# Four graph layers on one core: zero products ahead of layer 0, the branch moved behind the last store, layer 0's first loads into idle places

## The chip, the cores and the metric

The kernel runs on one core of a Trainium2 chip. The metric is device microseconds of one execution, from start to end of the program. Three runs of the kernel before took 511.5, 512.31 and 513.35 us; the median is 512.31 us.

## The reference

Four layers run one after the other over one dense matrix `adj` of 3327 x 3327 (float32, most of it zero) and node features `x` of 3327 x 64. Each layer computes new features, adds them to the old ones, and normalises each row.

```python
def _layernorm(x, axis=-1, eps=1e-5):
    m = jnp.mean(x, axis=axis, keepdims=True)
    v = jnp.var(x, axis=axis, keepdims=True)
    return (x - m) / jnp.sqrt(v + eps)
...
# layer 0
neigh = jnp.matmul(adj, features)
deg = jnp.sum(adj, axis=1, keepdims=True) + 1.0
neigh = neigh / deg
data = jnp.concatenate([features, neigh], axis=-1)
return jnp.matmul(data, W.T)
...
# layer 1: each pair (i, j) of nodes has a factor of its own
log_ij = _logmap(x[:, None, :], x[None, :, :], c)
agg = jnp.einsum('ij,ijc->ic', w, log_ij)
transformed = agg @ weight + bias
...
# layer 2
h_neigh = (adj @ X + X) / deg
...
# layer 3: only the last 100 neighbours of a row count, each half as much as the next
mask = (adj != 0).astype(support.dtype)
rank = jnp.cumsum(mask, axis=1)
w = mask * jnp.where(pos > 0, DECAY ** (k - pos), 0.0)
out = w @ support + bias
```

## The kernel before

The nodes are padded to 3328 = 26 blocks of 128. The transposed matrix is stored in four column chunks of 832 targets, and each chunk in 13 pairs of source blocks; one load brings one pair (128 partitions x 2 x 832 float32, 832 KB) into one of four buffers named `adj`. A layer thus reads 52 pairs. Loads are issued by SyncE (SP) in program order, each as soon as its buffer is free.

Layer 0 goes through the chunks in the order 0, 3, 1, 2, and through the pairs of a chunk from 12 down to 0. For each pair TensorE does four aggregating products (`aggregate_pair`, L488; the profile counts two matmuls for each) of the features `x0w` with the pair, into one PSUM bank. VectorE turns the pair into a 0/1 mask (L514). For the chunks 0, 1 and 2 TensorE then counts the nonzeros along the sources (`count`, L560, twelve bfloat16 products into two PSUM tiles), ScalarE writes the counts as bytes into `rank` (L570), and VectorE carries the last count into the next mask (L546); layer 3 needs these ranks. Six masks of chunk 0 are left over (`L0_SPILL`) and counted while chunk 3, which has no count in layer 0, is aggregated. `heads` says ahead of which pairs the own features of the blocks are made: `own_features` (L692) multiplies up to seven blocks of `xt` by the weights and ScalarE copies the result to `x0w` and `xr` (L698, L699). The seven small weight loads (`load_weights`, L205 to L211) are issued by SP when chunk 0 has reached pair 7.

When a chunk is aggregated, its sums are copied (`keep_sums`, L471), transposed back by TensorE (L603) and worked into new features by `sums0` and `features0`, a step at a time beside the pairs of the next chunk; `transposes0` (L671, L677, L678) then brings them into `ut` and `wt`, the two operands of layer 1. For the last chunk `sums0` runs at once behind the pairs, on VectorE alone (L606 to L623), `features0` inside layer 1.

Behind layer 0 VectorE sums up how many nodes are too near to the origin for a short formula (L796), TensorE adds over the partitions (L798), VectorE writes the integer `n_near` (L799), and all engines load it and branch (L1657, L1659): at zero to `layer1_far` and layers 2 and 3, otherwise to `layer1_near` and a second copy of layers 2 and 3. The first two pairs of layer 1 are loaded ahead, into `sums`.

In `layer1_far` two blocks at a time are worked on: TensorE makes the inner products (L858), VectorE multiplies with the matrix (L869), ScalarE squares and adds a constant (L882, L883), GpSimd (POOL) multiplies (L884) or, for fewer of the blocks, VectorE does the last two steps in one (L877), and TensorE aggregates (L889), six blocks behind. The steps of the late `features0` of the last chunk are put between these. Layers 2 and 3 follow; `epilogue3` makes the last rows and SP stores them (L1543, L1548). A scheduler of the framework orders the instructions of each engine by the order of the program and its own estimate; `issue_after` pins one behind another.

## Time and profile before

| | |
|---|---|
| the profiled execution, its own time | 514.65 us |
| its span | 512.9 us |
| TensorE busy | 471.0 us (92%) |
| VectorE busy | 382.7 us (75%) |
| ScalarE busy | 345.3 us (67%) |
| POOL busy | 214.8 us (42%) |
| granted TensorE clock, mean | 0.989 |
| read from memory | 130.88 MB, 257 GB/s over the span |

The profiled execution is 2.3 us longer than the median of the timed runs. Times below are microseconds from the start of its span. PE is TensorE, DVE VectorE, ACT ScalarE, POOL GpSimd, SP SyncE; SPq and POOLq are the instructions that issue loads and stores. Layer 0's chunks end at about 44, 73, 107 and 149 us, layer 1 at about 343, layer 2 at about 465; the rest is layer 3, whose early part lies among layer 2. The engines' busy shares are means over these stages; what a change is worth is read in its own stage.

### The profile page before, as it was taken

What the parts mean: (1) busy time and instruction counts of PE and PEld (TensorE: products, weight loads), DVE (VectorE), ACT (ScalarE), POOL (GpSimd) and SP (SyncE); (2) the same over time, 40 slices, a digit from 0 to 9 for tenths busy, and PEclk for the clock granted to TensorE, in tenths of its full rate; (3) what the DMA queues carried; (4) which work ended last, traced back from release to release, by engine and by line L of the source; (5) the groups of instructions that cost most, each with busy time, mean ns of one, the idle gap of its engine ahead of it and who ended that gap; (6) DMA issues with size and microseconds to landing.
All of it is one profiled execution on the core that took longest, in us unless ns stands there. A gap on an engine that the chain in (4) does not pass through costs nothing.

```text
span 512.9 us, 7870 instructions
## 1 busy us (share of the span) xinstructions
PE 471.0 (92%) x2888; PEld 240.0 (47%) x2888; DVE 382.7 (75%) x690; ACT 345.3 (67%) x432; POOL 214.8 (42%) x191
## 2 busy tenths in 40 slices
PE   5999899998967999999999999999999998999892
PEld 3454344453432333443353344354465545466782
DVE  3475429969867989889979987988789487836773
ACT  1455546776777998879977986921278846569882
POOL 2000201102108996769866995900412043420563
PEclk9999999999998999999999999999999999999997
DMA  8899999988829778867876878579969888970003
GB/s 274 289 386 335 389 385 354 339 293 265 305 67 306 252 260 265 266 209 226 266 245 216 253 267 267 195 272 404 327 202 356 305 293 331 315 277 2 0 0 75
DMA packets 46289, 132.49 MB, mean 258 GB/s; under 512 B 7046, under 2 KB 7150, under 8 KB 46178
## 3 DMA queue, kind: packets, MB, share of 16 engines
q1 hardware_dynamic: 45714, 131.36, 74.7%
q0 software_dynamic: 384, 0.52, 0.4%
q8 instruction: 24, 0.39, 0.3%
q14 instruction: 23, 0.19, 0.1%
q10 hardware_dynamic: 144, 0.03, 0.0%
HBM read 130.88 MB, written 0.85 MB: 257 GB/s over the span
## 4 chain that ended last, share of the span: by engine, by line
PE 55%; DVE 20%; ACT 11%; DMA 7%; issue 3%; POOL 2%; POOLq 0%; DVEq 0%; ACTq 0%
PE one L488 13%; PE two L858 11%; PE one L889 10%; DMA adj<-in_adjt_dram 6%; PE two L560 5%; DVE mask L546 4%; PE two L488 4%; ACT s L882 3%; ACT s L883 3%; DVE mask L514 3%; PE two L1463 3%; DVE p L869 2%; DVE exponents L1362 2%; DVE s L877 2%; PE two L926 1%
## 5 line engine op out<-in xcount | busy, mean ns | idle before, releaser
L884 POOL TENSOR_TENSOR s<-s,p 128x832 f32<-128x832 f32 x70 | 135.5, 1956 | 34.7 <-DVE p L869 21.1
L869 DVE SCALAR_TENSOR_TENSOR p<-two,adj 128x832 f32<-128x832 f32 x100 | 101.7, 1020 | 15.0 <-issue 11.1
L570 ACT ACTIVATE rank<-two,last_bias 128x832 uint8<-128x832 f32 x78 | 71.9, 952 | 45.5 <-PE two L560 23.8
L858 PE MATMUL two<-uw 64*128 64x416 f32 x416 | 89.8, 546 | 8.7 <-DVE s L877 3.9
L889 PE MATMUL one<-s,xu 128*64 128x416 f32 x416 | 86.2, 525 | 0.0
L488 PE MATMUL one<-adj,x0w 128*64 128x416 f32 x416 | 82.6, 524 | 2.6 <-ACT x0w L698 1.4
L882 ACT ACTIVATE s<-two 128x832 f32<-128x832 f32 x70 | 60.1, 860 | 27.5 <-DVE p L869 27.0
L546 DVE SCALAR_TENSOR_TENSOR mask<-two,minus_last,mask 32x832 bf16<-32x832 f32 x48 | 52.5, 1093 | 32.9 <-PE two L560 28.9
L858 PEld LDWEIGHTS two<-uw 64*128 64x128 f32 x416 | 37.6, 188 | 60.5 <-PE one L889 16.9
L514 DVE TENSOR_SCALAR mask<-adj 128x1664 bf16<-128x1664 f32 x48 | 50.7, 1056 | 18.3 <-DMA adj<-in_adjt_dram 17.5
L883 ACT ACTIVATE s<-s 128x832 f32<-128x832 f32 x70 | 62.6, 897 | 1.8
L560 PE MATMUL two<-mask,tri 128*64 128x416 bf16 x416 | 53.1, 345 | 7.2 <-DVE mask L546 5.1
L488 PE MATMUL one<-adj,xr 128*64 128x416 f32 x264 | 54.5, 518 | 1.2 <-DMA adj<-in_adjt_dram 1.0
L889 PEld LDWEIGHTS one<-s,xu 128*64 128x64 f32 x416 | 26.0, 136 | 48.1 <-issue 41.7
L488 PEld LDWEIGHTS one<-adj,x0w 128*64 128x64 f32 x416 | 29.3, 139 | 34.5 <-issue 23.8
L560 PEld LDWEIGHTS <-tri 128*64 128x64 bf16 x416 | 25.8, 111 | 39.8 <-issue 24.4
L1384 ACT ACTIVATE bits<-rank 128x832 fp32r<-128x832 uint8 (+1 forms) x42 | 38.7, 986 | 6.2 <-PE one L488 3.6
L1380 POOL TENSOR_SCALAR bits<-exponents 128x832 fp32r<-128x832 bf16 (+1 forms) x20 | 24.4, 1237 | 37.1 <-PE one L1463 19.3
L877 DVE SCALAR_TENSOR_TENSOR s<-two,p 128x832 f32<-128x832 f32 x34 | 34.6, 1018 | 0.8 <-ACT two L874 0.5
L1463 PE MATMUL two<-bits,parts 128*128 128x416 f32 x144 | 30.7, 359 | 2.0 <-POOL bits L1380 2.0
L874 ACT ACTIVATE two<-two 128x832 f32<-128x832 f32 x34 | 28.8, 847 | 4.4 <-DVE p L869 3.6
L570 ACT ACTIVATE uw<-two,last_bias 128x832 uint8<-128x832 f32 x26 | 24.2, 950 | 11.1 <-PE two L560 5.9
(311 smaller groups left out, 538.0 us busy)
## 6 DMA issues: line engine op xcount, KB each, us to landing
adj<-in_adjt_dram SPq DMA_DIRECT2D x135, 832.0 KB, 6.0
uw<-in_adjt_dram SPq DMA_DIRECT2D x7, 832.0 KB, 6.1
a<-in_adjt_dram SPq DMA_DIRECT2D x8, 416.0 KB, 6.7
sums<-in_adjt_dram SPq DMA_DIRECT2D x2, 832.0 KB
p<-in_adjt_dram SPq DMA_DIRECT2D x4, 416.0 KB, 6.5
s<-in_adjt_dram SPq DMA_DIRECT2D x4, 416.0 KB, 7.5
uw<-in_xt_dram SPq DMA_DIRECT2D x1, 640.0 KB
out_dram<-o SPq DMA_DIRECT2D x2, 192.0 KB, 2.9
```

The source lines that it names most:

```text
L488: issued = nc.tensor.matmul(acc[h * D : (h + 1) * D, 0:HC], lhsT=x[:, 2 * jp + k, 0:D], rhs=a[:, bass.ts(h, HC)], start=(first and k == 1) ...
L514: issued = nc.vector.tensor_scalar(mask, a2, 0.0, None, op0=ALU.not_equal)
L546: ranks.carried = nc.vector.scalar_tensor_tensor(halves(last), ranks.after[P - 32 : P, :, 0:HC], minus_last[P - 32 : P, :], halves(last), ...
L560: issued = nc.tensor.matmul(counts[k][rows, h, 0:HC], lhsT=lhsT[:, rows], rhs=mask[:, of, bass.ts(h, HC)], start=lhsT is tri, stop=(k == 1 ...
L570: ranks.made = nc.scalar.activation(halves(ranks.rank[:, 2 * jp + k, :]), counts[k][:, :, 0:HC], AF.Relu, bias=last_bias,)
L858: issued = nc.tensor.matmul(v[:, h, 0:HC], lhsT=wt[rows, bass.ts(jb, P)], rhs=ut[rows, bass.ds(c * CH + h * HC, HC)], start=True, stop=True,)
L869: issued = nc.vector.scalar_tensor_tensor(halves(p), v, 0.25 - 0.5 * FD, halves(a), op0=ALU.add, op1=ALU.mult)
L882: nc.scalar.activation(halves(s), v, AF.Square, bias=FB - 0.5, scale=-2.0)
L883: nc.scalar.activation(s, s, AF.Copy, bias=FG)
L884: nc.gpsimd.tensor_mul(s, s, p)
L889: issued = nc.tensor.matmul(acc[h * D : (h + 1) * D, 0:HC], lhsT=xu[:, jb, 0:D], rhs=s[:, bass.ts(h, HC)], start=first, stop=last,)
L1463: issued = nc.tensor.matmul(acc3[c][h][:, 0:HC], lhsT=parts[:, 2 * jp + b, :], rhs=bits[b][:, bass.ts(h, HC)], start=(c not in begun and b ...
```

## The change

- Thirteen bfloat16 products of a zero tile, 128 x 416 each, are put on TensorE ahead of everything else; VectorE clears the tile first.
- Own features: two blocks and four blocks ahead of pairs 12 and 11 as before, then four blocks at a time, each behind the aggregation of a pair (10, 8, 6, 4, 2), into the PSUM bank `one1` in place of the tiles that the counts use.
- The pairs 8 to 0 of chunk 0 are loaded into places that are idle then (`sums`, the `wt` half of `uw`, and parts of `rank` of the chunks 1 and 2), so that these nine loads wait for no buffer. `load_weights` moves to POOL's queue.
- Spilled masks: the number left grows from 1 in place of 0, to 6 as before.
- `transposes0` of a chunk in layer 0 goes in two parts (four blocks, then the others) through the bank of the chunk's sums.
- For the last chunk, the addition of `xr` and the squares in `sums0` go to POOL; its small tiles lie in PSUM.
- `vote` (the former L796 to L799) comes at the end of `layer1_far`. The far way always runs; only behind the last store is `n_near` loaded and branched on, and at a nonzero count the near way computes all from layer 1 on again. For that `xr` is kept in memory by a store of 832 KB on POOL's queue in layer 1 (`kept_x1`), and the PSUM banks are opened once for all layers.
- In the last `epilogue3` the root lies in PSUM in place of SBUF.

```diff
+L0_IDLE = 13
...
     def load_weights():
-        nc.sync.dma_start(out=w1s, in_=w1)
-        nc.sync.dma_start(out=w2s, in_=w2.rearrange("(t k) f -> k t f", t=2))
+        nc.gpsimd.dma_start(out=w1s, in_=w1)
+        nc.gpsimd.dma_start(out=w2s, in_=w2.rearrange("(t k) f -> k t f", t=2))
...
+    kept = ctx.enter_context(tc.tile_pool(name="kept", bufs=1, space=bass.MemoryType.DRAM))
+    kept_x1 = kept.tile([P, NB, D], FP, name="kept_x1")
...
-        (nc.vector if last else nc.gpsimd).tensor_add(y, y, xr[:, b0:b1_, 1:D])
-        ss = ss_last[:, 0:nb] if last else Work(nb)("ss")
-        yield sum_of_squares(y, nb, ss, last)
+        nc.gpsimd.tensor_add(y, y, xr[:, b0:b1_, 1:D])
+        ss = work("ss")
+        yield sum_of_squares(y, nb, ss, nc.gpsimd if last else False)
...
+    far = ExitStack()
+    banks = Banks(far, "psum_far")
     with ExitStack() as l0s:
-        banks = Banks(l0s, "l0psum")
...
+        zeros = setup.tile([P, HC], BF, name="zeros")
+        nc.vector.memset(zeros, 0.0)
+        idle = banks.pair(1)
+        for _ in range(L0_IDLE):
+            nc.tensor.matmul(
+                idle[:, 0, 0:HC], lhsT=zeros[:, 0:P], rhs=zeros, start=True, stop=True
+            )
...
         def own_features(b0, b1_, behind):
             nb = b1_ - b0
-            ps = per_block(places.free(), nb, 2 * D)
+            ps = per_block(banks.one(1), nb, 2 * D)
...
-        heads = {12: (24, 26), 11: (20, 24), 9: (13, 20), 6: (6, 13), 2: (0, 6)}
+        heads = {12: (24, 26), 11: (20, 24)}
+        ahead_of_use = {10: (16, 20), 8: (12, 16), 6: (8, 12), 4: (4, 8), 2: (0, 4)}
...
+        rooms = [sums, wt] + [
+            rank[:, c, :, :].rearrange("p b i -> p (b i)").bitcast(FP) for c in ORDER[2:]
+        ]
+        rooms = [room[:, bass.ts(k, 2 * CH)] for room in rooms for k in range(room.shape[1] // (2 * CH))]
+        rooms = [room.rearrange("p (b i) -> p b i", b=2) for room in rooms]
+
+        def load_early(jps):
+            for jp in jps:
+                loaded[jp] = load_adj(ORDER[0], jp, rooms.pop(0) if jp < 9 else None)
+
+        load_early((9, 8))
...
+                if n == 0 and jp in ahead_of_use:
+                    issued = own_features(*ahead_of_use[jp], issued)
...
-                left = (L0_SPILL - jp // 2 if ranks else jp // 2) if n < 2 else L0_LAG
+                left = (min(L0_SPILL, L0_SPILL + 1 - jp // 2) if ranks else jp // 2) if n < 2 else L0_LAG
...
-                        transposes0(ORDER[n - 1], places.free(), counted or issued, True)
+                        for k0, k1 in ((0, 4), (4, GB)):
+                            bank = banks.one((n - 1) % 2)
+                            transposes0(ORDER[n - 1], bank, counted or issued, True, k0, k1)
...
+                if n == 0 and jp == 10:
+                    load_early((7, 6, 5, 4))
+                    load_weights()
                 if n == 0 and jp == 7:
-                    load_weights()
+                    load_early((3, 2, 1, 0))
...
-        vote = banks.one(NCH % 2)
-        nc.tensor.matmul(vote[0:1, 0:1], lhsT=nearest, rhs=ones, start=True, stop=True)
-        nc.vector.tensor_copy(n_near, vote[0:1, 0:1])
...
+    def vote(bank, behind):
         nearest = small.tile([P, 1], FP, name="nearest", tag="nearest")
         nc.vector.tensor_reduce(nearest, near, axis=AX.X, op=ALU.add)
+        issue_after(nc.tensor.matmul(bank, lhsT=nearest, rhs=ones, start=True, stop=True), behind)
+        nc.vector.tensor_copy(n_near, bank)
...
+                    if late is None and i == late_at:
+                        nc.gpsimd.dma_start(out=kept_x1, in_=xr)
...
-                own = {"ss": "s", "root": "a", "part": "var"} if ends_with else {}
-                def work(name, work=Work(nb)):
+                own = {"ss": "vn", "part": "var"} if ends_with else {}
+                def work(name, work=Work(nb, bank if ends_with else None)):
...
+    with far:
+        layers_2_and_3(banks, *layer1_far(banks))
     some_near = nc.values_load(n_near[0:1, 0:1], min_val=0, max_val=NP)
-    with tc.If(some_near == 0) as cmp:
-        with ExitStack() as arm:
-            banks = Banks(arm, "psum_far")
-            layers_2_and_3(banks, *layer1_far(banks))
-    with cmp.Else():
+    with tc.If(some_near > 0):
         done = layer1_near()
```

## The prediction

> **What bounds the kernel now.** I read the busy time by stage first, then the chain that ended last, then the order of time at four places. By stage (us, then busy us and count of PE, PEld, DVE, ACT, POOL, then granted clock, DMA share, GB/s):
>
> ```profile
> 0.00:16.00 16.00, 10.17 (x46) 5.82 (x48) 5.22 (x15) 4.15 (x7) 3.44 (x35) 1.00 0.88 291
> 16.00:44.00 28.00, 26.60 (x196) 14.33 (x194) 18.15 (x35) 12.96 (x19) 0.74 (x5) 1.00 0.94 328
> 44.00:73.00 29.00, 27.37 (x196) 12.64 (x194) 11.03 (x29) 16.85 (x21) 3.45 (x4) 1.00 1.01 381
> 73.00:107.00 34.00, 32.51 (x252) 15.56 (x250) 29.43 (x47) 22.67 (x28) 4.16 (x4) 1.00 0.97 342
> 149.50:168.00 18.50, 10.41 (x44) 4.31 (x46) 13.83 (x27) 12.07 (x15) 12.53 (x12) 0.91 0.86 286
> 168.00:344.00 176.00, 172.85 (x905) 73.20 (x905) 154.31 (x251) 143.65 (x181) 133.58 (x70) 1.00 0.75 244
> ```
>
> Chunk 3 (44 to 73) runs at the rate of the loads, 381 GB/s at a full share; chunk 0 moves only 291 and 328 GB/s. So a lead of the loads in chunk 0 is a lead through chunk 3. From 168 on TensorE is the bound. Between them, at 149.5, it stands. The chain of waits (start, us, what) says where:
>
> ```profile
> 11.73 2.08 PE two L560 x12
> 16.70 1.07 PE two L560 x12
> 17.80 1.10 DVE mask L546
> 18.92 0.95 ACT rank L570
> 19.88 0.43 ACT x0w L698
> 56.51 7.67 DMA adj<-in_adjt_dram
> ...
> 151.00 0.62 DVE ss_last L430
> 151.65 0.18 DVE near_nodes L615
> 151.84 0.19 DVE nearest L796
> 152.03 0.04 issue
> 152.08 0.20 PE one L798 x2
> 152.31 0.16 DVE n_near L799
> 152.46 1.14 issue
> 153.61 2.99 PE two L858 x8
> ```
>
> Twelve count products take 2.08 us at 11.73 and 1.07 later: the array is slow until about 13.6, and again at 153.61, where eight L858 take 2.99 against 1.6 elsewhere (granted clock 0.91 in that stage). At 17.8 own features wait behind a count for ScalarE. At 149.5 the last count product is done, and the first product of layer 1 begins at 153.61, behind the vote and the branch.
>
> **Part by part.** *Zero products.* One L560 pair takes 0.35 us slow, and I take a full-width product of 416 columns to be as long as such a pair (no row shows one): 13 x 0.35 = 4.5 us, from about 1.1 to 5.6, just ahead of the first own features at 5.83, which wait for VectorE's `w0r`, not for TensorE. Cost nothing, unless they run over. What they can save by 13.6: eight L488 at 2.97 against 1.40 and the 2.08 against 1.07, together 2.6 us. But the loads land at 6.3, 8.5, 10.9 and 16.0 there, and TensorE, once fast, waits for them. So I book no term of its own; it is inside the next one. [...]
>
> *Chunks 0 and 3.* In the trace pair 9 lands at 16.0, pair 0 of chunk 0 at 39.7, the last pair of chunk 3 at 70.6. Before, loads wait for one of four buffers, and SP spends 15.77 to 19.6 on weight loads:
>
> ```profile
> 11.77 3.95 SPq L311 DMA_DIRECT2D adj<-in_adjt_dram  x2
> 15.77 0.48 SPq L205 DMA_DIRECT2D w1s<-in_w_dram  x1
> ```
>
> With nine pairs free to go, loads follow at the rate of chunk 3 (45.7 to 70.6 for 11 pairs: 2.26 us a pair): pair 0 at 16.0 + 9 x 2.26 = 36.3, chunk 3's last at 65.7. TensorE from 16.0: ten pairs x 1.40 + six counts x 1.05 + 16 own blocks x 0.126 + 0.5 = 22.8, so 38.8; chunk 3 is 13 x 1.40 + 6 x 1.05 + 1.3 = 25.8, so 64.6 and with stalls about 66. Both meet near 66 to 67.1 (65.7 + 1.4) against about 72 (70.6 + 1.4). Own features in fours take away the waits on ScalarE at 17.8 to 20.3 and 37.0 to 37.5. Gain 5.5; bounds 3.5 (pair 0 no earlier than 36.3, none of it added in chunk 3) and 7. Chunks 1 and 2 have loads, masks and counts as before; a phase earlier, the same length.
>
> *Transposes in layer 0.* TensorE waits 0.64 and 0.85 us on ScalarE's copies at 104.6 and 143.0, and up to 1.7 at 69.1. Their own bank lets counts go on; ScalarE's second pair of copies adds some 0.3 a chunk. Gain 1.0; bounds 0 and 2.3.
>
> *POOL's queue in layer 0.* Seven weight loads and three last-row loads stand at its front, the reads of `rank` rows between its steps. A POOL issue took 0.5 to 0.7 us mostly, once 3.68, and a POOL addition twice its 0.93 beside L514:
>
> ```profile
> 117.61 1.98 POOL L612 TENSOR_TENSOR y<-y,xr 128x441 f32<-128x441 f32 x1 [21.23 <-DVE y L611]
> 130.37 0.93 POOL L647 TENSOR_TENSOR xu<-y,a 128x441 f32<-128x441 f32 x1 [4.45 <-DVE a L645]
> 360.53 3.68 POOL L591 DMA_DIRECT2D rank<-last_more  x1 [26.34 <-DVE last_more L589]
> ```
>
> Ten issues at the worst of these are 37 us, at 0.6 six; POOL's next work in before is at 41.6, and the weights are first read by VectorE at 36.2, behind pair 2's mask, which the lead brings to about 33. So the front costs nothing in the likely case (third rival). The read of chunk 1's rows waits for ScalarE's last count of chunk 1 (117.9) and is queued ahead of L612 at 117.61: VectorE's sum behind it already waits 0.49 there. Cost 0.4; bounds 0 and 0.9.
>
> [...]
>
> *Layer 1's start.* The vote and branch leave: 149.5 to 153.61 on TensorE is 4.1 us, and the slow restart 1.4. In their place stands a chain on POOL: ScalarE's last count (151.1), the read of the rows (0.51), the addition and the squares (0.93 each with VectorE idle; 1.98 beside L514, which is over by then), so 153.6. VectorE's sum of the squares (0.62) stands between the first and second L869, so every later L869 waits for it: second L869 done 155.3, near steps 0.35, third 156.7, fourth 157.7 against 159.66. ScalarE (1.75 a block) then ends block five's L874 at 163.15 against 165.2, VectorE's L877 follows at 164.2 against 167.63, and with it TensorE's unbroken run at 164.4 against 167.77. Gain 3.4. Bounds: 1.5 if both POOL steps take 1.98 (+2.1), 5.0 if TensorE keeps all of 4.1 and most of the restart. The second load into `sums`, issued 148.9 behind four others, lands near 153.5, ahead of the third L869.
>
> *The store of `xr`* is one POOL issue behind the ninth L884, ahead of the tenth. POOL is back to back there (eight L884 in 15.34 us), but by then blocks lie some 5 us ahead of TensorE. Cost 0.2; bounds 0 and 3.7. Its 832 KB are 2.3 us of a queue at 0.75 share. *The vote* at layer 1's end: 0.2 on TensorE ahead of L912 and 0.16 on VectorE ahead of L903: 0.15 (0 to 0.4). SP's load of `n_near` (0.5 to 0.75) stands where SP waits 11 us for buffers (363 to 374.6): nothing, 0.7 at worst.
>
> *The end.* Here L449 takes 0.89 in place of 0.16, beside POOL:
>
> ```profile
> 505.40 0.94 POOL L1536 TENSOR_TENSOR o<-twice,root 128x448 f32<-128x448 f32 x1
> 505.46 0.89 DVE L449 TENSOR_TENSOR var<-var,a 128x4 f32<-128x4 f32 x1
> ```
>
> With the root in PSUM it may not; but SP issues stores until 508.2 and the last store's landing (512.0) ends the program, so SP must follow. Gain 0.5; bounds 0 and 1.2. The new branch on the four engines and on SP lies beside that landing (3.2 us); 0, a microsecond at worst.
>
> Sum: -5.5 - 1.0 + 0.4 - 3.4 + 0.2 + 0.15 - 0.5 = -9.65. Against the profiled 514.65 that is 505.0; that execution is 2.34 above the median, so 512.31 - 9.65 = 502.7.
>
> **Rivals.** *First: the loads in chunk 0 can't go faster.* Their share is already 0.88 and 0.94 at 291 and 328 GB/s; if small or narrow transfers, not the buffers, hold them down, only about 1 of the 5.5 comes. Against it: the same chunk moves 363 GB/s from 28 on, and is slow where buffers and SP run dry. 512.31 - 9.65 + 4.5 = 507.2. *Second: POOL's chain takes the vote's place.* If its issue and two steps run into 156 or later, the 3.4 falls to 0: 502.66 + 3.4 = 506.1. For it: the 1.98 row. *Third, the slower one: weights come late.* VectorE's queue holds `turn` of w1 ahead of the masks near 33; if POOL's issues, starved by L514, bring w1 to b3 only at 33 + 9.65 = 42.7 or later, the change is slower, by as much as they are later; at ten issues of 3.68 from 4.3 plus 8 us of landing (the longest POOL row), 49: about 6 slower, 518.6. Against it: three last-row loads landed in 6 us each beside four running pairs, with issues of 0.5 to 0.7. *Fourth: the large terms do nothing* (first and second together, and chunk 3 keeps its pace): within 0.3% of 512.3.
>
> **How the numbers follow.** Forecast as summed, within 499 to 505: 0.54. First rival 0.16, second 0.16, third 0.06, fourth 0.03, slower by several bounds at once 0.02, faster than 499 (large bounds together: -7 - 2.3 - 5 - 1.2 = 496.8) 0.03. The range of 8 in 10 takes in the first two rivals and half of the rest: 498.5 to 509.5. About 0.3% (1.5 us) is what a measurement of this kernel can tell from no change. Faster by more than that: 0.54 + 0.16 + 0.16 + 0.03 = 0.89; same 0.03; slower 0.08.
>
> **What would show it.** Right: pair 0 of chunk 0 lands near 36 and chunk 3's last near 66; twelve L560 take 1.05 from the first; no gap over 1 us on TensorE at layer 0's end, clock 1.00 there; second L869 done near 149 (155.3 less the 6.1 of layer 0), layer 1 ending some 9 us earlier than 343; L449 at 0.16 in the last rows. Wrong: chunk 1 beginning no earlier than 70 (72 before), a long DVE wait on POOL or on a weight load near 33, or layers 2 and 3 longer than 169 us, where I book nothing and the scheduler has reordered some counts.

## The result: 1.4% slower

The changed kernel took 520.88 us (median of six runs), the kernel before 513.06 us beside it: a ratio of 1.0143, with a 95% interval of 1.0101 to 1.0185. I had forecast 502.7. The execution profiled was the longest of the six, 526.26 us with a span of 524.5; it is a slow run (mean granted clock 0.969, the five others 0.977 to 0.987), which the ratio leaves out. So the trace is read for where time went, and the ratio for how much.

The stages of the changed kernel, in the columns of the first view of before (us, then busy us and count of PE, PEld, DVE, ACT, POOL, then granted clock, DMA share, GB/s):

```profile
16.00:44.00 28.00, 24.29 (x172) 12.15 (x169) 17.98 (x34) 13.69 (x23) 0.61 (x4) 1.00 1.03 390
44.00:77.00 33.00, 30.85 (x206) 14.39 (x207) 11.82 (x29) 17.19 (x23) 3.60 (x5) 0.95 0.79 287
157.00:168.00 11.00, 8.34 (x28) 2.84 (x28) 8.07 (x19) 9.07 (x12) 9.27 (x6) 0.69 0.21 71
405.00:440.00 35.00, 31.17 (x188) 16.32 (x185) 23.89 (x45) 20.22 (x29) 10.61 (x12) 1.00 0.92 325
440.00:474.00 34.00, 33.62 (x181) 18.20 (x179) 17.52 (x39) 21.36 (x22) 9.31 (x10) 0.95 0.65 227
```

Chunk 0's loads do run faster, 390 GB/s in place of 328. The lead is then thrown away: chunk 3 moves 287 GB/s where it moved 381. And the granted clock, 1.00 from 13.9 us on in before except for one short stretch and the last rows, is under 1.00 in three of these five.

The clock itself shows where part of the time goes. In all traces here it changes only at multiples of 3.413 us after its first change (in before after 41, 1 and 102 of them, in the changed kernel after 12, 1, 33, 2, 52, 2, 26, 1, 15, 1 and 5). These are the stretches of the changed kernel just ahead of a slow stretch (one at half clock), and the slow stretches behind them (same columns):

```profile
41.49:44.90 3.41, 1.30 (x14) 0.89 (x16) 0.67 (x3) 2.32 (x4) 0.76 (x5) 1.00 1.01 382
44.90:48.31 3.41, 3.41 (x16) 1.50 (x14) 1.09 (x1) 1.42 (x2) 0.00 (x0) 0.50 0.10 37
157.54:160.96 3.42, 1.35 (x8) 0.30 (x4) 1.87 (x5) 1.97 (x3) 3.07 (x3) 1.00 0.35 141
160.96:167.78 6.82, 6.23 (x16) 2.20 (x16) 5.62 (x13) 6.76 (x9) 5.44 (x4) 0.50 0.08 11
437.43:440.84 3.41, 1.51 (x13) 1.31 (x12) 1.95 (x3) 1.44 (x4) 2.22 (x3) 1.00 0.54 209
440.84:444.26 3.42, 3.42 (x13) 1.36 (x14) 2.82 (x5) 2.89 (x5) 0.00 (x0) 0.50 0.02 5
492.05:495.46 3.41, 1.57 (x7) 1.05 (x6) 1.98 (x2) 2.60 (x2) 3.41 (x3) 1.00 0.00 0
495.46:498.88 3.42, 3.37 (x10) 3.22 (x11) 1.52 (x2) 0.95 (x2) 3.42 (x3) 0.50 0.00 0
```

TensorE was busy for 1.30, 1.35, 1.51 and 1.57 us of 3.41, under half, and the next stretch ran at half clock. Where TensorE is the bound, one such stretch costs about 1.7 us of products (an estimate: half of 3.41). I counted all full-clock stretches in the 20 traces of this study: of those with TensorE busy for less than half, 52 of 52 were followed by a slow one (7 of 7 in the profiles of before and of the change); between 0.50 and 0.55, 4 of 14; above 0.55, 8 of 2,794. One wait of 1.9 us (in the stretch from 437.43), or two of 0.97 and 0.86 us (in the one from 492.05), were enough. The changed kernel's profiled execution has seven slow stretches between its start and its last rows, the one of before has one.

The stages by marks that hardly depend on where a slow stretch falls, us each, for the profiled execution of each kernel (chunk ends at the first copy of the chunk's sums; layer 1's start up to its first aggregating product; "border" from its last one to layer 2's first; "rest" from the last L1267 to the end of the span):

| kernel | chunk 0 | chunk 3 | chunks 1, 2 | start of layer 1 | layer 1 | border | layer 2 | rest |
|---|---|---|---|---|---|---|---|---|
| before | 43.6 | 29.8 | 72.7 | 18.7 | 175.6 | 3.3 | 122.5 | 46.6 |
| the change | 47.8 | 31.4 | 72.2 | 16.5 | 174.8 | 5.8 | 127.4 | 48.6 |
| zeros alone | 45.9 | 30.1 | 72.4 | 18.7 | 175.6 | 3.3 | 121.8 | 47.3 |
| loads alone | 45.4 | 30.1 | 71.0 | 18.7 | 175.6 | 3.3 | 121.5 | 48.9 |
| branch alone | 48.0 | 30.9 | 71.5 | 15.5 | 176.1 | 5.4 | 125.5 | 47.3 |
| transposes and root alone | 43.5 | 29.9 | 72.6 | 19.9 | 175.6 | 3.5 | 122.6 | 47.6 |
| change, last rows' loads held | 46.5 | 30.2 | 72.2 | 14.4 | 180.2 | 5.8 | 125.2 | 48.6 |
| change, vote apart, weights later | 44.2 | 29.8 | 72.9 | 16.1 | 175.1 | 3.6 | 121.3 | 48.3 |
| change, all mends | 42.7 | 29.7 | 72.7 | 15.8 | 176.7 | 3.6 | 122.1 | 49.0 |

Three places lose: chunk 0 (+4.2) with chunk 3 (+1.5), the border with layer 2 (+7.4), and the rest (+1.9). One gains: the start of layer 1 (-2.2). The change with the last rows' loads held, an experiment below, is another profile of nearly the same kernel: it loses in the same places, and in layer 1 by its own edit.

In chunk 0 the order on TensorE (start, us, instruction, idle before it) shows the wait:

```profile
39.39 0.32 PE L728 MATMUL two<-w1h,basis 64*64 64x64 f32 x2
...
41.71 0.54 PE L566 MATMUL two<-mask,tri 128*64 128x416 bf16 x4 [0.23 <-DVE mask L552]
44.14 0.54 PE L566 MATMUL two<-mask,tri 128*64 128x416 bf16 x4 [1.88 <-ACT wl L743]
44.49 0.54 PE L566 MATMUL two<-mask,minus 128*64 128x416 bf16 x4
44.84 2.97 PE L494 MATMUL one<-rank,x0w 128*64 128x416 f32 x8
```

Pair 0 landed at 38.6, but its aggregation (L494) stands behind a count, and the count behind ScalarE's copies of the later weights (L728 wrote them into a pair of banks that the counts use). Then the clock was at half: 2.97 us for eight, where the eight at 39.87, at full clock, took 1.62.

### The profile page after: what moved, and what is told of

Read it like the earlier page. It is cut to its first block, busy times and chain, and to the rows that moved or that the text cites. A ratio compares the mean times of both kernels' runs of the same rounds, so it can differ in the third digit from the quotient of the medians.

```text
span 524.5 us, 7920 instructions
## 1 busy us (share of the span) xinstructions
PE 484.7 (92%) x2901; PEld 244.3 (47%) x2901; DVE 378.9 (72%) x690; ACT 346.9 (66%) x442; POOL 222.1 (42%) x201
## 4 chain that ended last, share of the span: by engine, by line
PE 54%; DVE 20%; DMA 8%; ACT 7%; issue 4%; SPq 2%; POOL 2%; POOLq 0%; DVEq 0%; ACTq 0%
PE one L494 13%; PE two L891 11%; PE one L922 9%; PE two L566 6%; DVE mask L552 4%; DMA adj<-in_adjt_dram 4%; PE two L494 4%; DMA rank<-in_adjt_dram 3%; DVE mask L520 3%; ACT s L915 3%; PE two L1499 3%; DVE p L902 2%; ACT s L916 2%; SPq L317 2%; DVE s L910 2%
## 5 line engine op out<-in xcount | busy, mean ns | idle before, releaser
L576 ACT ACTIVATE rank<-two,last_bias 128x832 uint8<-128x832 f32 x78 | 72.4, 952 | 47.4 <-DVE mask L552 33.6
L891 PE MATMUL two<-uw 64*128 64x416 f32 x416 | 91.8, 554 | 6.0 <-DVE s L910 2.9
L494 PE MATMUL one<-adj,x0w 128*64 128x416 f32 x344 | 72.3, 517 | 4.1 <-DMA adj<-in_adjt_dram 3.2
L891 PEld LDWEIGHTS two<-uw 64*128 64x128 f32 x416 | 37.1, 190 | 59.9 <-issue 28.4
L566 PE MATMUL two<-mask,tri 128*64 128x416 bf16 x416 | 57.3, 344 | 7.6 <-DVE mask L552 5.2
L494 PE MATMUL one<-adj,xr 128*64 128x416 f32 x264 | 56.5, 530 | 0.7 <-DMA adj<-in_adjt_dram 0.7
L520 DVE TENSOR_SCALAR mask<-adj 128x1664 bf16<-128x1664 f32 x39 | 41.7, 1072 | 18.9 <-DMA adj<-in_adjt_dram 18.4
L922 PEld LDWEIGHTS one<-s,xu 128*64 128x64 f32 x416 | 26.0, 136 | 48.6 <-issue 42.4
L494 PEld LDWEIGHTS one<-adj,x0w 128*64 128x64 f32 x344 | 26.0, 136 | 29.6 <-issue 19.4
L1499 PE MATMUL two<-bits,parts 128*128 128x416 f32 x144 | 32.4, 373 | 3.4 <-POOL bits L1416 2.0
L566 PE MATMUL two<-mask,minus 128*64 128x416 bf16 x208 | 31.8, 340 | 0.0
```

The source lines that it names most:

```text
L494: issued = nc.tensor.matmul(acc[h * D : (h + 1) * D, 0:HC], lhsT=x[:, 2 * jp + k, 0:D], rhs=a[:, bass.ts(h, HC)], start=(first and k == 1) ...
L520: issued = nc.vector.tensor_scalar(mask, a2, 0.0, None, op0=ALU.not_equal)
L566: issued = nc.tensor.matmul(counts[k][rows, h, 0:HC], lhsT=lhsT[:, rows], rhs=mask[:, of, bass.ts(h, HC)], start=lhsT is tri, stop=(k == 1 ...
L576: ranks.made = nc.scalar.activation(halves(ranks.rank[:, 2 * jp + k, :]), counts[k][:, :, 0:HC], AF.Relu, bias=last_bias,)
L891: issued = nc.tensor.matmul(v[:, h, 0:HC], lhsT=wt[rows, bass.ts(jb, P)], rhs=ut[rows, bass.ds(c * CH + h * HC, HC)], start=True, stop=True,)
L922: issued = nc.tensor.matmul(acc[h * D : (h + 1) * D, 0:HC], lhsT=xu[:, jb, 0:D], rhs=s[:, bass.ts(h, HC)], start=first, stop=last,)
```

## Experiments

**Each part alone, and the loads undone.** First, the zeros alone on the kernel before:

```diff
+        zeros = setup.tile([P, HC], BF, name="zeros")
+        nc.vector.memset(zeros, 0.0)
+        idle = banks.pair(1)
+        for _ in range(13):
+            nc.tensor.matmul(idle[:, 0, 0:HC], lhsT=zeros[:, 0:P], rhs=zeros, start=True, stop=True)
```

> The kernel before with the thirteen products of zeros and nothing else of the change. Theory L (the new order of layer 0's loads is what costs; the zeros only make the array fast early, at about 4 us instead of 13.9): the products of chunk 0 that took 2.97 us for eight take about 1.5 from 6 us on, but the loads set the pace, so the time is 510.5 to 513, chunk 1 begins at 70.5 to 72. Theory C (the loss of the change lies in slow-clock windows that follow short waits anywhere in the program, wherever the waits come from): the zeros change nothing behind 20 us, 511 to 514, with slow windows behind 20 us as before (one at layer 1's start and the end).

Measured: 515.69 us, ratio 1.0051 (1.0028 to 1.0074). The zeros cost. TensorE of this run, with what it waited for on VectorE and ScalarE:

```profile
14.29 1.80 PE L700 MATMUL two<-w0r,uw 64*128 64x128 f32 x14 [0.21 <-DMA uw<-in_xt_dram]
16.11 1.03 DVE L515 TENSOR_SCALAR mask<-adj 128x1664 bf16<-128x1664 f32 x1 [2.98 <-DMA adj<-in_adjt_dram]
17.17 1.09 DVE L547 SCALAR_TENSOR_TENSOR mask<-two,minus_last,mask 32x832 bf16<-32x832 f32 x1
18.30 0.95 ACT L571 ACTIVATE rank<-two,last_bias 128x832 uint8<-128x832 f32 x1 [3.58 <-DVE mask L547]
19.15 0.52 ACT L706 COPY x0w<-two 128x441 f32<-128x441 f32 x1
19.72 5.82 PE L489 MATMUL one<-adj,x0w 128*64 128x416 f32 x16 [3.64 <-ACT x0w L706]
```

The fast array had done all that it could by 16.1 us, waited 3.64 us, and its next sixteen products took 5.82 us at half clock; in before, slow until 13.9, the wait at that place was 0.84 and sixteen took 3.01. Pair 9 landed at 16.1, so TensorE itself did not wait for it, but for the own features: their copy stands on ScalarE behind that of a count, and this one behind VectorE's work, which did wait for pair 9. Chunk 0 ended 2.3 us later. Theory L was right that the loads set the pace, by this detour, and wrong that this makes early speed harmless.

Then the changed kernel with its loads undone:

```diff
-        heads = {12: (24, 26), 11: (20, 24)}
-        ahead_of_use = {10: (16, 20), 8: (12, 16), 6: (8, 12), 4: (4, 8), 2: (0, 4)}
+        heads = {12: (24, 26), 11: (20, 24), 9: (13, 20), 6: (6, 13), 2: (0, 6)}
...
-                loaded[jp] = load_adj(ORDER[0], jp, rooms.pop(0) if jp < 9 else None)
...
-        nc.gpsimd.dma_start(out=w1s, in_=w1)
+        nc.sync.dma_start(out=w1s, in_=w1)
```

> The changed kernel with layer 0's loading as before: four buffers and no early rooms, weights issued by SP, own features in groups of two to seven in a free pair of banks, the old allowance of waiting masks. Zeros, transposes by halves, the addition and squares on POOL, the vote and the branch at the end stay. Theory L: chunk 0 ends near 43.5 instead of 47.8 and chunk 1 begins near 72 instead of 77; about 5 us come back, 515 to 516.5. My prediction's reading (the loads are a gain of 5.5 and something else costs more): it becomes 5 us slower still, near 526. Theory B (the move of the vote and of the work at layer 0's end costs): 519 to 522, the start of layer 1 as late as in the changed kernel relative to chunk 1's begin.

Measured: 521.75 us, 1.0199 (1.0145 to 1.0253). Nothing came back: chunk 0 ended at 46.9, with a slow stretch behind a wait at 18 us. So undoing the loads alone gives nothing back, and theory B's range held; the zeros, and three loads that an experiment below turns up, were still there.

> The kernel before with only layer 0's loading of the change: loads into idle rooms, weights issued by POOL, own features in fours, one more waiting mask. No zeros, and vote, branch and layer boundaries as before. Theory L: chunk 0 ends 3 to 5 us later than in the kernel before, and with the array slow until 13.9 rather more; 516 to 519. My prediction's reading: chunk 1 begins at 66 to 68, 507 to 508.5. Theory B or C (this part is harmless by itself): 511.5 to 514.

The reverse edit on the kernel before measured 515.84 us, 1.0058 (1.0029 to 1.0086). The loads land earlier here, pair 0 at 37.1 against 39.7, and chunk 0 still ends at 45.4, behind a wait of 1.88 us for ScalarE's copy of the later weights.

The later weights moved out of chunk 0:

```diff
-                if n == 0 and jp == 2:
+                if n == 1 and jp == 10:
                     later_weights(mask)
```

> The changed kernel with one move: the work on the later weights (two products into a free pair of banks, its copies on VectorE and ScalarE) stands behind pair 10 of chunk 1 and not behind pair 2 of chunk 0. If the 1.88 us wait of a count on ScalarE's copy at 42.3 and the slow-clock window behind it (44.9 to 48.3) are what makes chunk 0 end late: chunk 0 ends at 43.5 to 45 instead of 47.8, chunk 1 begins at 73 to 74.5, and the time falls by 2.5 to 4 to 517 to 518.5. If TensorE's own work in chunk 0 and the later landing of its loads set it (products without a gap from 20.4 to 41.5 us): chunk 0 ends at 46.5 or later and the time is within 1 us of 520.9.

Measured: 517.47 us, 1.0111 (1.0069 to 1.0154). Chunk 0 ended at 43.9 in place of 47.8: the 1.88 us wait and the slow stretch behind it were what made it late. Yet 43.9 is no gain on 43.6, although all loads of chunk 0 had landed by 38.5. TensorE's own work fills chunk 0. The same kernel without the zeros:

> The run with the later weights moved, without the thirteen zeros. If the zeros pay once the loads run ahead: the array is slow until 11 to 14 us, chunk 0 ends 1 to 2.5 us later than 43.9, 518 to 520. If they cost here as they do alone (+0.5%, because the fast array runs out of loads and falls back for two windows): 515 to 516.5.

Measured: 518.14 us, 1.0128 (1.009 to 1.0167), chunk 0 at 44.2. Beside the early loads the zeros neither pay nor cost by what these runs can tell.

**The branch alone.** Vote, branch, POOL's addition and squares, store of `xr`, on the kernel before:

```diff
-        nc.tensor.matmul(vote[0:1, 0:1], lhsT=nearest, rhs=ones, start=True, stop=True)
...
+            own = banks.pair()
+            vote(own[0:1, 1, 0:1], summed)
...
-    some_near = nc.values_load(n_near[0:1, 0:1], min_val=0, max_val=NP)
-    with tc.If(some_near == 0) as cmp:
+    with far:
+        layers_2_and_3(banks, *layer1_far(banks))
+    some_near = nc.values_load(n_near[0:1, 0:1], min_val=0, max_val=NP)
+    with tc.If(some_near > 0):
```

> The kernel before with only the move of the vote, the branch and the work at layer 0's end (addition and squares of the last group on POOL, copy of its sums, store of xr, vote behind layer 1, branch behind the last store). No zeros, loads, transposes and last root as before. Theory M (several small prices, read off the first four runs): layer 1's start gains 2.4 to 3.4, the vote costs 1.0 at layer 1's end, layer 2 about 0.6 and often a slow-clock window of 1.7, the program's end 1.6; sum +0.5 to +2.5, so 512.5 to 515. The prediction's reading (-3.4 + 0.2 + 0.15, the branch beside the landing): 509.2. If the 6 us between the run with zeros alone and the run with loads undone are all of this part: 517 or more.

Measured: 518.65 us, 1.0124 (1.0094 to 1.0153), more than theory M allowed. It loses most in layer 0, whose code it shares with before until the last group. POOL's order of time, and TensorE's, in this run:

```profile
4.96 2.61 POOL L587 DMA_DIRECT2D last_a<-in_adjt_dram  x3
```

```profile
17.89 1.82 PE L698 MATMUL two<-w0r,uw 64*128 64x128 f32 x14
21.82 5.82 PE L491 MATMUL one<-adj,x0w 128*64 128x416 f32 x16 [2.11 <-ACT x0w L704]
```

In before these three loads of the last adjacency rows were issued from 153.9 on, right behind the branch. Without a branch ahead of them nothing held them, and they went to the front of POOL's queue, among layer 0's first pairs: pair 9 landed at 18.2 in place of 16.0, pair 7 at 22.7 in place of 20.3 (the expectation below calls it pair 8). TensorE waited 2.11 us and then ran 16 products in 5.82 us at half clock. The changed kernel has them at 10.50, behind its seven weight loads, and its pair 9 lands at 18.2 too.

So I held them back behind the store of `xr` in layer 1 (the fill of `last_more` likewise):

```diff
+            issued = nc.gpsimd.dma_start(out=a[k * NB : (k + 1) * NB, :], in_=adjt[c, :, P - 1, :])
+            issue_after(issued, held)
```

> The run with the move of the branch alone, and one thing more: POOL issues the three loads of the last adjacency rows (and the fill of the tile behind them) behind the store of xr, early in layer 1, in place of the first microseconds of the program, where they had slid once no branch stood ahead of them. Theory R (these loads lie among layer 0's first loads and delay them: pair 9 landed at 18.2 instead of 16.0, pair 8 at 22.7 instead of 20.3, TensorE waited 2.1 us and ran two slow windows): pair 9 lands near 16.0 again, chunk 0 ends at 43.5 to 45 instead of 48.0, chunk 2 at 146 to 147.5 instead of 150.4; 514 to 515.5 against 518.65. If the late chunk 0 of that run was chance: about 518 again. If POOL, back to back in layer 1, can't take six issues more: layer 1 lasts longer than 176.1 us.

Measured: 519.21 us, 1.0127 (1.0097 to 1.0157): the same time, by another way. Layer 0 is back, chunk 0 at 43.6 and chunk 2 at 144.3 in place of 150.4. But layer 1 lasts 179.3 in place of 176.1. POOL, and then TensorE:

```profile
176.24 1.97 POOL L889 TENSOR_TENSOR s<-s,p 128x832 f32<-128x832 f32 x1
178.13 0.53 POOL L589 DMA_DIRECT2D last_a<-in_adjt_dram  x1
178.66 0.51 POOL L592 DMA_DIRECT2D last_more<-rank  x1
179.18 1.96 POOL L889 TENSOR_TENSOR s<-s,p 128x832 f32<-128x832 f32 x1
```

```profile
185.71 1.67 PE L863 MATMUL two<-uw 64*128 64x416 f32 x8 [2.95 <-DVE s L882]
```

Six issues and a fill, some 4 us, now stand between POOL's back to back products, and TensorE waits 2.95 us where it had not waited. Of the 6.1 us won by the end of layer 0, 3.2 were lost again in layer 1. On the whole change the same hold:

> The changed kernel with the last rows' loads held back behind the store of xr and nothing else. Theory R: pair 9 lands near 16.8 instead of 18.2, pair 0 near 37.1 instead of 38.6; the count that waits for ScalarE's copy of the later weights at 42.3 still waits, so chunk 0 ends at 45 to 48; 518 to 520.5. If these loads are the greater part of the loss: 516 to 517.

Measured: 523.87 us, 1.0221 (1.02 to 1.0242). Chunk 0 at 46.5 as expected, the new wait in layer 1 (3.02 us at 186.7) as well. It is the slowest of all kernels here.

**The vote in a bank of its own**, on the change with the later weights moved (517.47 us).

```diff
-            own = banks.pair()
-            vote(own[0:1, 1, 0:1], summed)
-            own = own[:, 0, :]
+            vote(banks.one(0)[0:1, 0:1], summed)
+            own = banks.pair()[:, 0, :]
```

> The run with the later weights moved, and the vote's product in a bank of its own in place of the second bank of the pair in which the own part of layer 1's last group is computed. If TensorE's 0.81 us wait for VectorE's copy of the vote at layer 1's end is there only because both share one pair: the time from the last product of layer 1 to the first aggregation of layer 2 falls from 4.3 to about 3.5 us, and with it VectorE's chain in layer 2; 516 to 517 against 517.5. If something else holds the own part back: 4.3 again and 517.5.

Measured: 516.11 us, 1.008 (1.005 to 1.011). TensorE at the border, in the changed kernel and then in this run:

```profile
342.64 0.19 PE L845 MATMUL two<-ones,nearest 128*1 128x1 f32 x2
343.64 1.78 PE L945 MATMUL two<-w1r,uw 64*128 64x64 f32 x14 [0.80 <-DVE n_near L846]
```

```profile
338.03 1.55 PE L945 MATMUL two<-w1r,uw 64*128 64x64 f32 x12
339.51 0.19 PE L845 MATMUL one<-ones,nearest 128*1 128x1 f32 x2
339.63 0.43 PE L945 MATMUL two<-w1r,uw 64*128 64x64 f32 x2
```

The wait for VectorE's copy of the vote goes, because nothing else is written to that bank. The time, 516.11 against 517.47, is not clear of noise, since the intervals of the two ratios overlap. What the shared pair had cost is more than the 0.8 us: over all profiles, layer 2 lasts 122.6 to 127.4 with the vote in the shared pair (seven kernels, mean 125.2), 120.8 to 123.3 with the vote apart (seven, mean 121.8), and 121.0 to 122.6 with the vote in its old place (six, mean 121.9). With the shared pair VectorE is late in layer 2: with the later weights moved, its L1331 (L1295 in before) starts 86.8 us after layer 1's last aggregating product, in before 84.8. TensorE waits for it, here in the changed kernel:

```profile
439.56 1.77 PE L1303 MATMUL two<-wl,sums 128*128 128x128 f32 x12 [1.90 <-DVE sums L477]
```

This wait leaves the stretch from 437.43 under half busy and brings the slow one at 440.84. It is 1.86 to 1.91 us in all seven kernels with the shared pair and at most 1.0 in the thirteen others; a slow stretch follows it in four of the seven and in none of the others. The one of the seven with no slow stretch at the border or in layer 2, the change without zeros, lasted 122.6 there, no longer than with the vote in its old place. By this one profile, most of the 3.4 us between the means is the clock's. On the branch alone, with the loads held:

> The same with the vote's product in a bank of its own. What was seen with the other loads (layer 1's last product to layer 2's first aggregation 3.6 instead of 4.3 us, and no slow window behind it): 0.8 to 2.5 us less than the run without, 512 to 514. If the wait for the vote costs nothing in the end: as that run.

Measured: 515.27 us, 1.0053 (1.0035 to 1.0071), 3.9 us less than without, and here the intervals lie apart.

And the whole change with the later weights moved, the vote apart and the loads held:

> The changed kernel with three mends: later weights behind pair 10 of chunk 1, the vote in a bank of its own, the last rows' loads held back behind the store of xr. Theory R: pair 9 lands at 16.5 to 17 instead of 18.1, pair 0 near 37, chunk 0 ends near 43, and the time falls by 1 to 2 from 516.1 to 514 to 515. If TensorE's own work and the four buffers of chunk 3 set layer 0 here: 516 again. My prediction's reading, that early loads are worth several us once nothing is in their way: 510 or less.

Measured: 516.22 us, 1.0077 (1.0058 to 1.0095). Chunk 0 ended at 43.3, chunk 2 at 146.2; layer 1 had the wait of the held loads. The early loads were still worth nothing.

**The loads where they had stood**, in POOL's idle 3.5 us behind the squares and ahead of layer 1, on the branch alone with the vote apart:

```diff
+            if alone is nc.gpsimd:
+                on_pool.append(squared)
...
-                    acc, rows = begin2(banks, loading, loaded2, done[-1])
+                    acc, rows = begin2(banks, loading, loaded2, done[-1], False, on_pool[0])
```

> The move of the branch alone with the vote in a bank of its own and the three loads of the last rows behind POOL's squares at layer 0's end, ahead of its first addition of layer 1. Theory R: chunk 2 ends near 144 to 146.5, layer 1 starts 2.4 to 3 us earlier than in the kernel before, no wait of TensorE over 1 us near 183, layer 1 lasts 175.5 to 176.5; the end costs 1.6; 511 to 513. If the move has a price that is still unnamed: 514 or more.

Measured: 516.85 us, 1.0083 (1.0054 to 1.0112). Layer 0 and layer 2 are those of before, the start of layer 1 is 3.2 us shorter, and layer 1 lasts 181.9. The price still unnamed was a VectorE instruction, L657. VectorE in order of time, and then POOL:

```profile
167.13 0.20 DVE L656 RECIPROCAL var<-om 128x7 f32<-128x7 f32 x1
167.25 0.97 DVE L878 SCALAR_TENSOR_TENSOR p<-two,adj 128x832 f32<-128x832 f32 x1
168.14 3.55 DVE L657 TENSOR_SCALAR xu<-var 128x7 f32<-128x7 f32 x1
```

```profile
160.17 11.49 POOL L893 TENSOR_TENSOR s<-s,p 128x832 f32<-128x832 f32 x6
```

128 x 6 or 7 numbers take 0.17 us in the other chunks. Here they took 3.55, ending with the sixth of POOL's multiplications; TensorE then waited 2.50 us and ran two slow stretches. The same instruction took 0.57 in before, 0.73 in the change, 1.7 in three of the other kernels and 3.6 in three. The 3.55 us span the ends of two of POOL's multiplications of 1.9 us each. In all 20 profiles this instruction of the last group ended within 0.04 us behind one of POOL's multiplications (in before at 170.95 and 170.92 us); what holds it up was not tried.

**All mends on the whole change**: later weights moved, vote apart, loads behind the squares, and the store of `xr` on SP:

```diff
-                        nc.gpsimd.dma_start(out=kept_x1, in_=xr)
+                        nc.sync.dma_start(out=kept_x1, in_=xr)
```

> The whole change with the later weights moved, the vote apart, the last rows' loads behind the squares and the store of xr issued by SP. If layer 0's early loads are worth nothing because TensorE's own work in chunk 0 and four buffers in chunk 3 hold layer 0: chunk 2 ends at 145.5 to 146.5, the time is that of the mended branch alone, 511 to 514. My prediction's reading (early loads worth several us): 508 or less.

Measured: 514.67 us, 1.0063 (1.004 to 1.0086), the best version of the change. Layer 0 ends at 145.1, within the 143.7 to 146.2 of the kernels whose layer 0 is that of before up to its last group. TensorE from pair 9 to the end of chunk 0 and in chunk 3, in before and then in this run (columns of the first view):

```profile
16.00:43.65 27.65, 26.25 (x192) 14.10 (x190) 18.15 (x35) 12.61 (x19) 0.74 (x5) 1.00 0.94 330
43.65:73.47 29.82, 28.19 (x202) 13.11 (x200) 11.50 (x29) 17.67 (x21) 3.45 (x4) 1.00 1.01 379
```

```profile
16.70:42.65 25.95, 25.54 (x188) 13.19 (x186) 18.78 (x32) 13.50 (x20) 0.00 (x0) 1.00 1.03 402
42.65:72.36 29.71, 28.59 (x200) 13.84 (x196) 11.92 (x33) 18.31 (x27) 4.17 (x9) 1.00 0.92 334
```

It was busy for 54.4 us there in before, and for 54.1 with the early loads: its own work fills the two chunks, whether the loads come early or not.

**Zeros in a wait.** In before, TensorE waits 2.6 us for the vote. Fourteen products of zeros fill it:

```diff
+        for _ in range(14):
+            issue_after(nc.tensor.matmul(
+                vote[:, 0:HC], lhsT=zeros[:, 0:P], rhs=zeros, start=True, stop=True
+            ), counted)
```

> The kernel before with fourteen products of zeros between the last count product of layer 0 and the vote's product, in TensorE's wait for VectorE (149.5 to 152.1 us), into the vote's own bank; nothing else waits for them. Theory C (a stretch of 3.41 us in which TensorE is busy for less than about half sets the clock to half for the next one): the slow window at 153.8 to 157.2 does not come, eight products there take 1.6 instead of 2.99 us, and the time from the end of layer 0's last sums to layer 1's unbroken run falls from 18.7 by up to 1.4; 510.8 to 512.2. If the slow window has another cause: it stays, and 512.2 to 512.8.

The stretch ahead of layer 1 and the next (columns of the first view), in before and then with the zeros:

```profile
150.41:153.82 3.41, 0.40 (x4) 0.33 (x6) 1.66 (x5) 0.67 (x1) 0.65 (x1) 1.00 0.53 216
153.82:157.24 3.42, 3.42 (x12) 1.73 (x10) 1.64 (x2) 0.73 (x1) 3.29 (x7) 0.50 0.84 247
```

```profile
150.01:153.42 3.41, 2.37 (x12) 1.22 (x12) 1.31 (x2) 0.20 (x1) 2.76 (x5) 1.00 0.41 95
153.42:156.84 3.42, 1.85 (x8) 0.60 (x8) 3.24 (x4) 3.40 (x5) 2.20 (x4) 1.00 1.03 387
```

The slow stretch is gone, so TensorE's own idleness is its cause; the mean granted clock of the runs rose from about 0.986 to 0.991. The start of layer 1 fell from 18.7 to 17.6. The time did not move beyond doubt: 511.86 us, 0.9991 (0.9972 to 1.001). Behind that wait ScalarE and VectorE set the pace of the first blocks: with the zeros they were busy for 3.40 and 3.24 us of the 3.42 from 153.42 on, TensorE for 1.85. In layer 1's start of the moved branch, ahead of the fourth block (`pad` is the idle bank `one0`), twelve zeros did worse (the first of the two kernels also has the store of `xr` on SP, which it had not without the zeros):

```diff
+                        if i == 3:
+                            pad = banks.one(0)
+                            for _ in range(12):
+                                ahead_of = nc.tensor.matmul(pad[:, 0:HC], lhsT=zeros[:, 0:P], rhs=zeros, start=True, stop=True)
+                                issue_after(ahead_of, v_issued)
```

> The same, with the store of xr issued by SP and twelve products of zeros in TensorE's wait of 2.3 us behind the first three blocks of layer 1. Theory C: no slow window at 152 to 159 us in most executions, four products of a block there take 0.97 us or less from the first; the stretch from the last sums of layer 0 to layer 1's unbroken run falls from 15.5-16.5 by 0.5 to 1.5; 510 to 512. If ScalarE and VectorE set that stretch, as in the kernel before with zeros ahead of the vote: the clock is better, the time is that of the run without.

> The same with twelve products of zeros in TensorE's wait at layer 1's start. Theory C: as there, 0.5 to 1.5 less than without, 510 to 513; otherwise the same time as without.

Measured: 519.04 us, 1.0146 (1.0118 to 1.0174), and 517.5 us, 1.0095 (1.0067 to 1.0124); without the zeros 516.85 and 514.67. Only the second kernel had a slow stretch at layer 1's start without the zeros (two, from 154.8); with them it is gone, and the start is 0.5 us shorter. The first had none, and its start is 0.3 longer. The instruction that was L657 took 3.58 us in both, also in the second, where it had taken 0.72 without the zeros, and that loses more than the clock wins. Why it takes 3.58 with the zeros was not tried.

**The last two parts alone.**

```diff
-                        transposes0(ORDER[n - 1], places.free(), counted or issued, True)
+                        for k0, k1 in ((0, 4), (4, GB)):
+                            bank = banks.one((n - 1) % 2)
+                            transposes0(ORDER[n - 1], bank, counted or issued, True, k0, k1)
...
-                own = {"ss": "s", "root": "a", "part": "var"} if ends_with else {}
+                own = {"ss": "vn", "part": "var"} if ends_with else {}
```

> The kernel before with two parts of the change alone: layer 0's transposes in two halves in the bank of the group's sums, and the last root's inputs in PSUM. The prediction's reading: chunk 3's end to chunk 2's end shrinks by 1.0 from 71 to 72.7 us, the last rows by 0.5; 510.2 to 511. Reading by the traces of the change: waits on VectorE's masks take the place of those on ScalarE's copies, the stretch lasts 71.5 to 73 us, and the end is not set by VectorE; 511.5 to 513.

> The same with fourteen products of zeros between the last count of layer 0 and the vote, as in the run with these zeros alone (511.86, 0.1% less than before, not to be told from it). If the two parts gain: 509.5 to 510.5. If not: 511.3 to 512.5.

Measured: 515.22 us, 1.006 (1.0038 to 1.0082), and 514.64 us, 1.0047 (1.0027 to 1.0067) with the zeros ahead of the vote. Over all profiles chunks 1 and 2 last 71.0 to 72.7 us without the halves (nine kernels, mean 71.7) and 71.6 to 73.4 with them (eleven, mean 72.6), so the halves cost some 0.8, though the ranges overlap. These two chunks in before, and then with the halves (columns of the first view):

```profile
73.47:146.20 72.73, 67.67 (x526) 33.15 (x524) 58.92 (x93) 50.47 (x63) 8.92 (x8) 1.00 0.84 292
```

```profile
73.30:145.90 72.60, 69.51 (x527) 33.86 (x525) 58.99 (x92) 51.03 (x67) 9.36 (x8) 1.00 0.84 292
```

The waits on ScalarE, 1.5 to 1.7 us in every kernel without the halves, are gone, but TensorE is busy longer with the same products: 67.3 to 67.7 us in all nine without, 68.9 to 69.8 in all eleven with them. With the halves its products change from one source line to another 79 times in place of 53, in the changed kernel product by product from 148.05 on; that this is what makes them longer was not tried. Layer 1's start was 19.9 and 18.8 us, against 18.7 in before and 17.6 with the zeros alone: 1.2 more in each, with one slow stretch more than its counterpart there. The last rows end no earlier. The rest of this pair's 2 to 3 us I can't place.

No version was faster than the kernel before by more than the runs can tell.

## Why the prediction was wrong, step by step

- *Zero products.* Booked at nothing, with a gain of at most 2.6. The thirteen take 3.79 us, where I had put 4.5, end at 4.99 and delay nothing, as said. That products of zeros bring the full clock early was my assumption, which no row of before showed; in the change it is granted from 3.9 us on, in before from 13.9. But the step asked only what a fast array saves, not what it does when it runs dry: alone they cost 0.5%.
- *Chunks 0 and 3* (-5.5) is the step that failed most, and in it TensorE's own work. I had summed it to 22.8 us from pair 9 to the end of chunk 0 and to 25.8 in chunk 3, 48.6 together; it was busy for 54.1 in the version with all mends and for 54.4 of 57.5 in before. What the sum left out, 5.5, is as much as the gain that I booked: the lead was never there to win. I took 16 own blocks at one product of 0.126; a block has two, and the traces show 1.16 us for four blocks, 4.6 in place of 2.0. The other 2.9 are not traced to single terms. Two more terms made the change slower than before there. The loads: pair 9 lands at 18.2, not 16.0, and nine pairs later pair 0 at 38.6; the rate of 2.26 us a pair was right, its starting point was not, for the weights (0.8: 16.7 with the loads alone) and the last rows' loads (1.4 more). The counts: pair 0 waited behind a count that waited for the later weights. Chunk 0 ended 4.2 later, and so chunk 3's four buffers came free late; its loads paused from 47.1 to 50.6 us. I named "chunk 1 beginning no earlier than 70" as the sign of failure; chunk 3's sums are copied at 79.2.
- *Transposes* (-1.0): the waits on ScalarE went as said, but I booked nothing for TensorE's own products, which took 1.8 us longer in the run with the halves and the root alone; over all profiles the stretch is 0.8 longer.
- *POOL's queue in layer 0* (+0.4, "the front costs nothing"): I priced what the issues cost POOL, and not what their transfers cost the pairs beside them. In the change the ten issues took 0.5 to 1.2 us each; the longest, 1.23 at 6.29, lay beside a mask of VectorE, as the 3.68 of before did. The weights themselves came in time: VectorE read them at 36.7, so the third rival was wrong in its mechanism, though right in its sign.
- *Layer 1's start* (-3.4, bounds 1.5 to 5.0): right within its bounds. 2.2 us in the profile of the change, 2.3 to 4.3 in the other kernels with the moved branch. In the profile of the change POOL's addition took 1.13 us and its squares 0.92, the latter with VectorE idle; the 0.93 of before, which I put to an idle VectorE, lay beside an L546 (130.32 to 131.41). The second rival fell.
- *The store of `xr`* (0 to 3.7): right for the change; with the branch alone layer 1 was 0.5 longer.
- *The vote* (+0.15, 0 to 0.4): wrong in size. 1.0 at the border, 2.1 to 2.5 where slow stretches fell there, and some 3.4 in layer 2, most of it by slow stretches. I counted the two instructions and not who waits for the copy: the next products write the same pair of banks.
- *Layers 2 and 3*, where I booked nothing: 169.1 us before, 175.9 after; my sign was "longer than 169". Of this, 4.9 lie in layer 2, with the shared pair's wait and two slow stretches, and 1.9 at the program's end.
- *The end* (-0.5): L449 took 0.16 in every profile with the new root, but also in two of nine with the old, and nothing ended sooner. *The branch* ("beside the landing, a microsecond at worst"): from the end of the last store's issue to the end of the span 3.7 to 4.8 us without it (six profiles, mean 4.0), 4.6 to 6.0 with it (fourteen, mean 5.2). It costs 1.2.
- The ground of the forecast: the profiled execution of before was 2.3 us above its median, and its layer 0 ended at 146.2 where other kernels with the same code there had 143.7 to 145.7. Part of the waits that I meant to save was chance.

The parts do not add up: alone they cost 0.5, 0.6, 1.2 and 0.6%, a sum of 2.9%, where the whole change costs 1.4%. Layer 0's losses overlap, since one late chunk 0 has several causes. With all mends 0.6% remains; of it the halves of the transposes (0.8 us) and the end (1.2 us) are named, set against a gain at layer 1's start. The rest stays open.

## What to carry to other kernels

Taking away a branch also takes away a fence: look for what had stood behind it and is now free to go first, loads above all, and price their transfers beside the running ones, not only their issue (here three loads went from 153.9 to 4.96 us, and pair 9 landed 2.2 us later). When a small result shares a bank with the next stage's products, the wait for its copy (0.80 us here) belongs to the price. Where TensorE's clock follows its own busy share, as in these traces, sum the waits within each few microseconds: two side by side of 0.97 and 0.86 us were followed by a stretch at half clock, as one of 1.9 us was. And before booking a gain for earlier loads, add up how long the engine behind them is busy in the same stretch of the trace: where that is nearly all of it (54.4 of 57.5 us here), there is nothing to win.

## What I had not expected of the hardware

- The clock: a full-clock stretch of 3.413 us with TensorE under half busy was followed by a slow one 52 times of 52. Three kernels with the vote in the shared pair had two slow stretches at the border, behind one that began at 341.8 to 342.8 us with a busy share of 0.76, and two kernels with the vote elsewhere had one there, behind a stretch with TensorE busy throughout; the count does not explain these.
- A VectorE instruction on 128 x 7 numbers took between 0.17 and 3.58 us; the long ones all ended just behind an instruction of POOL.
- Three loads that POOL issues in 2.6 us moved a pair of 832 KB by 2.2 us, in the kernel with the branch alone.
